# Four norms' residual rows in the middle turns: added by accumulating DMAs from GpSimd's queue instead of VectorE

## The chip, the cores and the metric

The kernel runs on one core of a Trainium2 chip. A core has TensorE (PE, matrix products), VectorE (DVE), ScalarE (ACT), GpSimd (POOL) and SyncE (SP). Each works through its own queue in order; semaphores tie the queues together. SP, ACT and POOL can issue DMAs, which 16 DMA engines carry out. The metric is the device time in microseconds (us) of one execution; several executions give a median. A separate profiled execution gives the page and the trace.

## The reference

A batch of 64 graphs with 256 nodes and 256 features, in float32, passes through two layers. Layer 0 is a graph attention layer with two attention steps; layer 1 is multi-head attention in which the adjacency matrix selects one of two value projections. Each layer ends in a feed-forward part, and each has two layer norms.

```python
# layer 0
h = _gat(x, adj, W1, a1, Fout)
h = _gat(h, adj, W2, a2, W2.shape[1])
h = _layernorm(residual + h, g_ln1, b_ln1)
residual2 = h
ff = jnp.matmul(jax.nn.relu(jnp.matmul(h, w_ff1) + b_ff1), w_ff2) + b_ff2
return _layernorm(residual2 + ff, g_ln2, b_ln2)
...
# layer 1
x = _ln(src + attn_out, g1, beta1)
ff = jax.nn.gelu(x @ W1 + b1, approximate=False) @ W2 + b2
return _ln(x + ff, g2, beta2)
```

A layer norm here is (x - mean) / sqrt(variance + eps), times a row g, plus a row b. There are four norms in all.

## The kernel before

**Tiles.** Two graphs make one unit, so there are 32 units. A unit's rows are a tile `y` of 128 partitions x 4 blocks x 256 float32 numbers, that is 512 KB. The pool has four such buffers.

**Norms.** What a norm feeds on goes two ways. The normalised rows, without g and b, are transposed and go into the next product, whose weights have g and b folded in. The residual path needs the rows with g and b. So after a norm `y` is normalised in place (L855 on ACT, L852 on GpSimd for two blocks of one of the norms), VectorE transposes it (L694), and later VectorE multiplies `y` by the row g (`times`, L864) and adds the row b (`plus`, L867), each as one instruction of 128 x 1024 elements. The rows rb1, rb2 and rb3 also hold the bias of the product that follows, which is added to the same residual. Then the products' results are added into `y` from PSUM: L995 for a feed-forward part, L814 for an attention.

**Turns.** `turn(u, u + 1, u + 2)` runs 32 times and works at once on three units at different stages: Y (`y_`) in layer 1, X (`x_`) in the second half of layer 0, and Z (`z`) in the first half of layer 0. Z exists in turns 0 to 29. A fourth unit, the one whose layer 1 ended in the turn before, is in `waiting`: its last norm is finished in this turn and its rows are stored. So each middle turn applies four pairs of g and b:

- rg1, rb1 to X's rows after its first norm (L1343, L1344); next read by the first L995 of X's feed-forward part.
- rg4, rb4 to the waiting rows (L1419); next read by the store to HBM (`stored`, L1202, on SP).
- rg3, rb3 to Y's rows after layer 1's first norm (L1444); next read by the first L995 of Y's feed-forward part, late in the same turn.
- rg2, rb2 to X's rows after layer 0's last norm (L1490); next read by L814 in the next turn.

**Order.** Inside a turn the order on PE, SP, VectorE and ACT is the order of the code (`manual_schedule`). GpSimd's order is chosen by the scheduler. SP issues, in this order within a turn: 12 DMAs that place transposed features (`hT<-yt`, L713) for X's first norm, 8 loads of x (L436), 6 more L713 (ACT issues another 6), the store of the waiting rows (L1202), the load of new rows into the buffer just stored (L441), 12 DMAs L703 for the next transposed features, and 8 loads of the adjacency (L449). GpSimd, in a turn, computes reciprocal square roots (`rs`, L837 and L838), copies the diagonal blocks of the transposed features (L711, L703), normalises two blocks (L852), and keeps small running checks (L780, L840, L1125). The products of a feed-forward part are done by a seven-product scheme over quarters (class `HiddenOut`), whose sums of quarters (L973) and additions into `y` (L995) are VectorE's. The softmax of Z (L768, L775, L779) and the scaling of its features by `z` (L791, ACT) lie in the same stretches; the product `ygp` (L811) uses them.

Of the kernel before, what the change touches and what calls it, by code (L numbers as in the profile page):

```python
# [12 lines left out]
ALU = mybir.AluOpType  # L13
# [372 lines left out]
def narrow_path(  # L386
# [13 lines left out]
    nc = tc.nc  # L400
# [102 lines left out]
    def row(v, name, t=None):  # L503
        n = v.shape[0]
        if t is None:
            t = const.tile([P, n], F32, name=name)
        nc.sync.dma_start(t, bass.AP(tensor=v.tensor, offset=v.offset, ap=[[0, P], [1, n]]))
        return t
# [41 lines left out]
    rg1, rb1, rg2, rb2 = row(g_g1, "rg1"), row(g_b1, "rb1"), row(g_g2, "rg2"), row(g_b2, "rb2")  # L550
# [14 lines left out]
    rg3, rb3, rg4, rb4 = row(t_g1, "rg3"), row(t_be1, "rb3"), row(t_g2, "rg4"), row(t_be2, "rb4")  # L565
# [289 lines left out]
            mark["normed"] = nc.scalar.activation(y[:, t, :], y[:, t, :], AF.Identity,  # L855
                                                  bias=nm[:, t:t + 1], scale=rs[:, t:t + 1])

    def affine(y, g_, b_):

        times(y, g_)  # L860
        plus(y, b_)

    def times(y, g_):
        nc.vector.tensor_mul(y, y, g_[:, None, :].to_broadcast(list(y.shape)))  # L864

    def plus(y, b_):
        nc.vector.tensor_add(y, y, b_[:, None, :].to_broadcast(list(y.shape)))  # L867

    def hidden_seven(u, l, hT, w, bi, func, d, tt):

# [135 lines left out]
    class Projections:  # L1006
# [17 lines left out]
        def out(s, x, o, b):  # L1024
            if x == "q":
                return s.qk[:, o, :, b * N:(b + 1) * N]
            return s.v[:, b * NB:(b + 1) * NB, o * F:(o + 1) * F]
# [172 lines left out]
    def stored(u, y, bt):  # L1200
        b = slice(G * u + bt.start // NB, G * u + bt.stop // NB)
        nc.sync.dma_start(out[b].rearrange("b (c p) f -> p (b c) f", p=P), y[:, bt, :])  # L1202

    def finish(u, y, b):

        normed(u, 3, y, range(b * NB, (b + 1) * NB))
        bt = slice(b * NB, (b + 1) * NB)
        affine(y[:, bt, :], rg4, rb4)
        stored(u, y, bt)
# [16 lines left out]
    def turn(y_, x_, z):  # L1226
        Y, X, Z = (g.get(u) for u in (y_, x_, z))
        hT, y = Y["hT"], Y["y"]
# [7 lines left out]
        def scores(n, heads=range(HPB)):  # L1236
            pe[n], e[n] = weighted(y_, *quads[n], q, k_, Y["aT"])
            powers(n, heads)
# [34 lines left out]
        with order:  # L1273
# [67 lines left out]
            first("4a 7b rb")  # L1341
            if X:
                times(X["y"], rg1)  # L1343
                plus(X["y"], rb1)  # L1344
            scores(3)
            first("sa sb", 2)
            masks(3)
# [64 lines left out]
            if not Z:  # L1412
                piece()
                hT = to_features(y, f"h3T{y_}")
                hT = [h.rearrange("p (t a r) -> p t a r", t=T, r=32) for h in hT]
                if not X:
                    affine(y, rg3, rb3)
            if waiting:
                affine(waiting[0][1], rg4, rb4)  # L1419
                stored(*waiting.pop(), slice(0, T))  # L1420
            if z + 1 < NG:
                load_rows(z + 1)
# [18 lines left out]
                offsets(*n)  # L1441
                applied_norm(X["y"], *n, [0])
            if Z:
                affine(y, rg3, rb3)  # L1444
            second("3a")
            if X:
                applied_norm(X["y"], *n, [1])
# [39 lines left out]
            Z["m"].shares()  # L1487
            Z["m"].scaled(F)
            out(3)
            affine(X["y"], rg2, rb2)  # L1490
            out(7)
            Z["n"] = norm(z, 0, Z["y"], mv=second_sums(z))
            out(4)
# [2 lines left out]
    waiting = []  # L1496

    with tc.manual_schedule(engines={mybir.EngineType.PE, mybir.EngineType.SP}):
# [34 lines left out]
        for u in range(NG):  # L1533
            turn(u, u + 1, u + 2)
# [54 lines left out]
```

## Time and profile before

| | us |
|---|---|
| median of 3 runs (lowest, highest) | 3045.75 (3045.45, 3047.17) |
| the profiled execution's own time | 3043.91 |
| its span in the trace | 3042.3 |
| one addition L867 of 128 x 1024, median | 1.226 |
| one multiplication L864 of 128 x 1024, median | 1.217 |
| DMA of 512 KB from SP, issue to landing: row load L441 / store L1202, median | 4.4 / 2.9 |
| DMA of 512 KB from GpSimd (L462, two at the start), issue to landing | 8.0 and 9.9 |
| time of those two on GpSimd's queue | 1.01 and 0.79 |

The page's rows give a group of instructions as line, engine, operation, tiles written and read, shape and count; then busy time in us and the mean of one in ns; then the idle time of the engine just before them and what ended most of it. The granted TensorE clock was 0.995 of full speed in the mean. A turn in the middle lasts about 92.4 us.

### The profile page before, as it was taken

To read this page: it belongs to the slowest core of one execution; us is meant where nothing else is said; L and a number is where in the kernel's file an instruction comes from. 1 tells how busy PE (TensorE), PEld (TensorE's weight loads), DVE (VectorE), ACT (ScalarE), POOL (GpSimd) and SP (SyncE) were. 2 spreads that over 40 slices of the span, in tenths; PEclk is the share of its full clock that TensorE was granted. 3 is DMA by queue.
4 is the path that set the end of the run, shared out by engine and by line. 5 is a ranking of instruction groups with operands and counts; after the bars stand their busy time and mean duration, and the time that the engine had idled before them with its cause. 6 is when DMAs were issued, how large, how long until landed. Compare 5 with 4: busy or idle time off the path is not lost.

```text
span 3042.3 us, 58414 instructions
## 1 busy us (share of the span) xinstructions
PE 3000.0 (99%) x22192; PEld 2459.6 (81%) x22192; DVE 2645.7 (87%) x5025; ACT 1684.9 (55%) x3404; POOL 679.8 (22%) x930
## 2 busy tenths in 40 slices
PE   7999999999999999999999999999999999999998
PEld 6788888888787888787888878887878887878876
DVE  5788988888898889898889888898988898988887
ACT  4455555655655555555555455556555555555553
POOL 4222221222211222212222112222112222122211
PEclk8999999999999999999999999999999999999999
DMA  5011111211111211111111112111112111121000
GB/s 147 13 35 36 37 39 25 44 37 39 34 35 32 44 37 39 33 27 43 40 37 36 40 25 44 38 39 33 34 35 44 36 38 35 25 45 37 19 13 16
DMA packets 428402, 113.24 MB, mean 37 GB/s; under 512 B 364586, under 2 KB 427604, under 8 KB 428116
## 3 DMA queue, kind: packets, MB, share of 16 engines
q1 hardware_dynamic: 418076, 102.20, 15.3%
q10 hardware_dynamic: 8984, 6.19, 0.8%
q8 instruction: 178, 2.92, 0.4%
q0 software_dynamic: 1056, 1.05, 0.1%
q14 instruction: 108, 0.88, 0.1%
HBM read 56.78 MB, written 16.78 MB: 24 GB/s over the span
## 4 chain that ended last, share of the span: by engine, by line
PE 90%; DVE 7%; ACT 1%; DMA 1%; POOL 1%; issue 0%; SPq 0%; DVEq 0%; POOLq 0%; ACTq 0%
PE yf L987 22%; PE h1a L898 15%; PE h1b L898 12%; PE po L1112 8%; PE qk L1053 7%; PE v L1053 7%; PE sp L1084 4%; PE xpp L740 4%; PE yop L811 4%; PE ygp L811 3%; PE zo L1115 2%; PE hpp L800 2%; DVE s L775 2%; DVE yt L694 1%; DVE eaq L973 1%; DVE y L995 1%
## 5 line engine op out<-in xcount | busy, mean ns | idle before, releaser
L907 ACT COPY h<-h1b 128x512 f32<-128x512 f32 x384 | 224.5, 585 | 349.4 <-PE h1b L898 342.6
L910 DVE TENSOR_TENSOR h<-h1a,h 128x512 f32<-128x512 f32 x384 | 262.9, 685 | 114.6 <-PE h1a L898 108.8
L1097 DVE TENSOR_TENSOR ea<-e,aT 128x1024 f32<-128x1024 f32 x256 | 311.2, 1237 | 2.9 <-ACT e L1093 2.6
L855 ACT ACTIVATE y<-y,nm,rs 128x256 f32<-128x256 f32 x450 | 249.8, 597 | 114.4 <-DVE nm L845 110.1
L1093 ACT ACTIVATE e<-sp 128x512 f32<-128x512 f32 x512 | 270.8, 600 | 28.1 <-PE sp L1084 21.4
L1036 ACT COPY qk<-qk 128x512 f32<-128x512 f32 x128 | 75.1, 587 | 339.0 <-PE qk L1053 339.0
L711 POOL COPY hT<-yt 32x256 f32<-32x256 f32 x244 | 203.2, 833 | 184.9 <-DVE yt L694 172.6
L837 POOL TENSOR_SCALAR rs<-mv 128x4 f32<-128x4 f32 (+1 forms) x134 | 33.3, 248 | 841.0 <-DVE mv L827 625.3
L826 DVE BATCH_NORM_STATS2 st<-y 128x6 f32<-128x256 f32 x512 | 207.3, 407 | 4.5
L995 DVE TENSOR_TENSOR y<-yf,y 128x256 f32<-128x256 f32 x448 | 183.2, 409 | 29.5 <-PE yf L987 29.4
L1125 POOL TENSOR_TENSOR low<-low,rq 128x16 f32<-128x16 f32 x64 | 13.9, 218 | 810.4 <-DVE rq L1124 810.4
L867 DVE TENSOR_TENSOR y<-y,rb 128x1024 f32<-128x1024 f32 (+1 forms) x130 | 167.0, 1284 | 3.2
L941 ACT ACTIVATE h<-h,cols 128x512 f32<-128x512 f32 x256 | 167.0, 714 | 1.5 <-DVE h L910 1.1
L864 DVE TENSOR_TENSOR y<-y,rg 128x1024 f32<-128x1024 f32 (+1 forms) x130 | 161.6, 1243 | 1.2 <-ACT y L855 1.1
L1102 DVE TENSOR_TENSOR es<-e 128x1024 f32<-128x1024 f32 x128 | 155.8, 1217 | 0.0
L703 POOL COPY hT<-yt 32x256 f32<-32x256 f32 x120 | 114.9, 958 | 169.3 <-DVE yt L694 165.1
L838 POOL TENSOR_TENSOR rs<-rs,mhalf 128x4 f32<-128x4 f32 (+1 forms) x134 | 146.9, 1096 | 8.3
L1084 PE MATMUL sp<-qk 32*128 32x256 f32 x2048 | 146.6, 400 | 0.4 <-DVE qk L1040 0.3
L742 ACT COPY xp<-xpp 128x260 f32<-128x260 f32 x128 | 45.4, 385 | 172.6 <-PE xpp L740 172.5
L694 DVE STREAM_TRANSPOSE yt<-y 128x256 f32<-128x256 f32 x364 | 136.0, 418 | 4.5
L1112 PE MATMUL po<-e,v 128*32 128x256 f32 x2048 | 136.3, 384 | 0.0
L898 PE MATMUL h1a<-tt,wf 128*128 128x256 f32 x512 | 134.2, 386 | 0.3 <-DVE h L910 0.3
(280 smaller groups left out, 7589.6 us busy)
## 6 DMA issues: line engine op xcount, KB each, us to landing
hT<-yt SPq DMA_DIRECT2D x912, 32.0 KB, 1.9
y<-in_x_dram SPq DMA_DIRECT2D x32, 512.0 KB, 4.5
xq<-in_x_dram SPq DMA_DIRECT2D x240, 64.0 KB, 2.1
aq<-in_adj_dram SPq DMA_DIRECT2D x240, 64.0 KB, 2.3
out_dram<-y SPq DMA_DIRECT2D x30, 512.0 KB, 2.9
hT<-yt ACTq DMA_DIRECT2D x180, 32.0 KB, 1.9
wf<-in_L_gnn_w_ff_dram SPq DMA_DIRECT2D x2, 1024.0 KB, 7.6
w<-in_L_gnn_W_dram SPq DMA_DIRECT2D x2, 1024.0 KB, 7.9
```

Source lines behind the costliest of these rows:

```text
L811: nc.tensor.matmul(ps[:, i * F:(i + 1) * F], lhs(t, k), rhs(b, k), start=(k == 0), stop=(k == n - 1))
L855: mark["normed"] = nc.scalar.activation(y[:, t, :], y[:, t, :], AF.Identity, bias=nm[:, t:t + 1], scale=rs[:, t:t + 1])
L898: nc.tensor.matmul(ps[:, i * N:(i + 1) * N], w_[:, f * P:(f + 1) * P], m, start=first and i == 0, stop=True, skip_group_check=True)
L907: mark["copied"] = nc.scalar.copy(out(h, o, b), pair(ps))
L910: mark["added"] = nc.vector.tensor_tensor(out(h, o, b), pair(one[h]), out(h, o, b), ALU.add)
L987: nc.tensor.matmul(s.ps[n][:, i * F2:(i + 1) * F2], a[:, k, i * P:(i + 1) * P], w_[:, k, :], start=n in (1, 2, 5) and i == 0 and k == 0, s ...
L995: mark["out"] = nc.vector.tensor_tensor(yq, s.ps[n][:, :F].rearrange("p (i f) -> p i f", i=NB), yq, ALU.add)
L1053: nc.tensor.matmul(ps[:, i * N:(i + 1) * N], l, r, start=n in (1, 2, 5) and i == 0, stop=True, skip_group_check=True)
L1084: nc.tensor.matmul(ps[a][:, j * N:(j + 1) * N], k_[hp, m, j0:j0 + P], q[hp, m, b * N:(b + 1) * N], start=True, stop=True)
L1093: nc.scalar.activation(e[:, a, :], ps[a], AF.Exp, scale=isd)
L1097: nc.vector.tensor_tensor(ea[:, a:a + 2, :], e[:, a:a + 2, :], ab[:, None, :].to_broadcast([P, 2, NB * N]), ALU.mult)
L1112: nc.tensor.matmul(po[hp, m * N:(m + 1) * N], vs[:, hp], w[:, a, j * N:(j + 1) * N], start=(n == 0), stop=(n == len(terms) - 1))
```

## The change

In turns that have a Z, the addition of the row b to `y` is a DMA that accumulates into `y`, issued from GpSimd's queue, in place of VectorE's `tensor_add`. Its source is the row tile of 128 x 256, read four times over. It applies to rb1, rb2, rb3 and rb4. The multiplications by g stay on VectorE. Turns 30 and 31, the part ahead of the turns and the halves of the last units (`finish`) keep VectorE's addition.

```diff
--- before.py
+++ after.py
@@ -855,16 +855,20 @@
             mark["normed"] = nc.scalar.activation(y[:, t, :], y[:, t, :], AF.Identity,
                                                   bias=nm[:, t:t + 1], scale=rs[:, t:t + 1])
 
-    def affine(y, g_, b_):
+    def affine(y, g_, b_, queue=False):
 
         times(y, g_)
-        plus(y, b_)
+        plus(y, b_, queue)
 
     def times(y, g_):
         nc.vector.tensor_mul(y, y, g_[:, None, :].to_broadcast(list(y.shape)))
 
-    def plus(y, b_):
-        nc.vector.tensor_add(y, y, b_[:, None, :].to_broadcast(list(y.shape)))
+    def plus(y, b_, queue=False):
+        rows_ = b_[:, None, :].to_broadcast(list(y.shape))
+        if queue:
+            nc.gpsimd.dma_start(y, rows_, accum_op=ALU.add)
+        else:
+            nc.vector.tensor_add(y, y, rows_)
 
     def hidden_seven(u, l, hT, w, bi, func, d, tt):
 
@@ -1341,7 +1345,7 @@
             first("4a 7b rb")
             if X:
                 times(X["y"], rg1)
-                plus(X["y"], rb1)
+                plus(X["y"], rb1, Z is not None)
             scores(3)
             first("sa sb", 2)
             masks(3)
@@ -1416,7 +1420,7 @@
                 if not X:
                     affine(y, rg3, rb3)
             if waiting:
-                affine(waiting[0][1], rg4, rb4)
+                affine(waiting[0][1], rg4, rb4, Z is not None)
                 stored(*waiting.pop(), slice(0, T))
             if z + 1 < NG:
                 load_rows(z + 1)
@@ -1441,7 +1445,7 @@
                 offsets(*n)
                 applied_norm(X["y"], *n, [0])
             if Z:
-                affine(y, rg3, rb3)
+                affine(y, rg3, rb3, True)
             second("3a")
             if X:
                 applied_norm(X["y"], *n, [1])
@@ -1487,7 +1491,7 @@
             Z["m"].shares()
             Z["m"].scaled(F)
             out(3)
-            affine(X["y"], rg2, rb2)
+            affine(X["y"], rg2, rb2, True)
             out(7)
             Z["n"] = norm(z, 0, Z["y"], mv=second_sums(z))
             out(4)
```

## The prediction

> **What bounds the kernel now.** I read the page first (shares, and the chain that ended last), then the busy time by windows, then TensorE's waits, and last one middle turn on every engine in order of time.
>
> ```profile
> span 3042.3 us, 58414 instructions
> PE 3000.0 (99%) x22192; PEld 2459.6 (81%) x22192; DVE 2645.7 (87%) x5025; ACT 1684.9 (55%) x3404; POOL 679.8 (22%) x930
> PE 90%; DVE 7%; ACT 1%; DMA 1%; POOL 1%; issue 0%; SPq 0%; DVEq 0%; POOLq 0%; ACTq 0%
> L867 DVE TENSOR_TENSOR y<-y,rb 128x1024 f32<-128x1024 f32 (+1 forms) x130 | 167.0, 1284 | 3.2
> ...
> 120.00:2860.00 2740.00, 2735.54 (x20419) 2245.89 (x20418) 2436.08 (x4612) 1546.53 (x3132) 603.54 (x824) 1.00 0.17 36
> ...
> PEld yf L987 <- DVE eaq L973: 15.0, 30, 0.5
> ```
>
> The windows line gives length, then busy time of PE, PEld, DVE, ACT and POOL. TensorE leaves only 2740.00 - 2735.54 = 4.5 us uncovered over the 30 middle turns that the change touches. VectorE, 87% busy, enters the chain at one place in a turn: a quarter sum (eaq, L973) that a product waits for, 0.5 us in each of 30 turns. One removed addition costs 1284 ns.
>
> Next, the turn from 1495.7 to 1588.1 us (VectorE, then GpSimd, then ACT and TensorE), and the transfers of the same size:
>
> ```profile
> 1530.56 1.22 DVE L867 TENSOR_TENSOR y<-y,rb 128x1024 f32<-128x1024 f32 x1
> 1544.68 0.42 DVE L995 TENSOR_TENSOR y<-yf,y 128x256 f32<-128x256 f32 x1
> 1548.25 0.42 DVE L995 TENSOR_TENSOR y<-yf,y 128x256 f32<-128x256 f32 x1 [0.48 <-PE yf L987]
> 1567.16 0.69 DVE L910 TENSOR_TENSOR h<-h1a,h 128x512 f32<-128x512 f32 x1 [1.00 <-PE h1a L898]
> 1575.74 0.41 DVE L995 TENSOR_TENSOR y<-yf,y 128x256 f32<-128x256 f32 x1
> ...
> 1552.10 4.40 POOL L711 COPY hT<-yt 32x256 f32<-32x256 f32 x4 [1.48 <-DVE yt L694]
> 1561.15 0.23 POOL L837 TENSOR_SCALAR rs<-mv 128x4 f32<-128x4 f32 x1 [4.65 <-DVE mv L827]
> 1563.64 2.95 POOL L852 TENSOR_SCALAR y<-y,rs,nm 128x256 f32<-128x256 f32 x2 [1.15 <-DVE nm L845]
> 1572.09 3.98 POOL L703 COPY hT<-yt 32x256 f32<-32x256 f32 x4 [5.50 <-DVE yt L694]
> ...
> 1581.65 1.71 ACT L791 ACTIVATE hp<-hp,z 128x256 f32<-128x256 f32 x4 [2.73 <-DVE z L779]
> 1582.84 3.62 PE L811 MATMUL ygp<-hp,s 128*128 128x256 f32 x16
> ...
> 2.87 0.79 POOL L462 DMA_DIRECT2D first<-in_adj_dram  x1
> ...
> out_dram<-y SPq DMA_DIRECT2D x30, 512.0 KB, 2.9
> first<-in_adj_dram POOLq DMA_DIRECT2D x2, 512.0 KB, 9.0
> ```
>
> The brackets are the idle time before an instruction and what ended it. VectorE waits for TensorE at 1548.25 and at 1567.16, so what it saves earlier in the turn turns into a longer wait there; from 1575.74 on it has no gap until after the masks, so a delay at that addition passes on. GpSimd has 4.65 and 5.50 us free where two of the new DMAs go.
>
> **What the Trainium skill says.** "DMA: Bandwidth & Descriptors", section "SWDGE vs HWDGE vs iDMA": an accumulating DMA can be issued from GpSimd alone, whose cores write its descriptors. No run shows such a DMA here; the plain ones of L462 occupied GpSimd for 0.79 and 1.01 us. "Perfetto Trace Analysis", section "DMA Instruction — SWDGE (GPSIMD)": that row ends when the descriptors are written, not when the data has landed. The trace agrees: rows of about 0.9 us, landing after 9.0. "Collectives: The Full Stack", section "The bandwidth ceiling: the fold count and why AG ≠ RS ≠ AR": an adding transfer reads two sources for each piece it writes and ran at half the copy's rate for that reason, not for the addition. No run here shows it. "SBUF — State Buffer", section "Who interferes with whom": a VectorE instruction with two SBUF inputs and a GpSimd instruction that reads SBUF block each other. The trace agrees: L852 takes 557 ns at its fastest and 1457 in the median.
>
> **The change part by part.** Turns 0 to 29 have a Z. Three norms (rb1, rb2, rb3) give 30 DMAs each, the fourth (rb4) needs a waiting result and gives 29: 119 of the 130 additions of L867 go, and 119 DMAs of 512 KB come. VectorE loses 119 x 1.284 = 152.8 us. The order of TensorE, ACT and SP is unchanged; VectorE's changes only in that the additions are gone and some short instructions around the turn's seam swap.
>
> Landing time of one such DMA, from GpSimd's start. From below: the store of the same size lands in 2.9 us. From above: a plain one from GpSimd took 9.9 us beside loads that filled the DMA engines (97% busy in the first 20 us); with a second read, 12. My value: 0.9 for descriptors, 2.9 as for the store, and once more the data time of 512 KB, which I estimate from the first page's "Anatomy of one DMA" (512 KB / 436 GB/s = 1.2): 5.0 us; 6 with other traffic. Time on GpSimd: 0.8 to 1.0 us by L462, up to 3 if the second read's descriptors are written one by one and more slowly; I take 1.
>
> rb1: multiplied until 1530.5, DMA right away (GpSimd is idle, an update of low waits behind it and nobody waits for that), landed at 1536.5; first reader is the L995 at 1544.68, 8 us later. The 1.22 us that VectorE saves here end in the wait at 1548.25. After it come only instructions that stay, up to eaq. Worth 0.
>
> rb4: GpSimd reaches it after the L711 copies at 1556.5. Behind it on GpSimd is the rs of L837 at 1561.15: free for 4.65 us, hidden. The store on SP waits for it: 1556.5 + 6 = 1562.5 instead of 1556.3; behind it on SP are the row load, which waits for the store to land (1562.5 + 2.9 = 1565.4 instead of 1559.1; its data is needed in the next turn), and then the transposed features' DMAs at 1572.0. They stay on time as long as the landing is under 1572.0 - 1556.5 - 2.9 - 0.4 (one issue) = 12.2 us. Worth 0; VectorE's gain ends in the wait for the features' DMAs at 1557.87 (L881).
>
> rb3: GpSimd reaches it after the two L852, at 1566.6, or some 0.9 sooner since the removed addition no longer blocks the second one (1457 to 557 ns). Behind it are the L703 copies, 5.5 us later. VectorE's gain ends in the wait at 1567.16. This landing has the nearest reader: L995 at 1575.74, 9.1 us after 1566.6. If it is late, z and the scaling at 1581.65 are, and with them ygp, whose second matmul (1582.84 + 0.22) needs the second scaled block (1581.65 + 2 x 0.43 = 1582.5): 0.5 us of slack. So nothing happens below 9.6 us, and beyond it TensorE loses the rest, 30 times. At 6 it is hidden, also when the later row load (1565.4 on) shares the engines and costs 1 to 2 us. Worth 0.
>
> rb2: multiplied until 1583.1, DMA then. Behind it is the rs of L837 at 1589.22, 6.1 us later. Landed near 1589; first reader is the attention's addition in the next turn, over 40 us later. VectorE gets to the moments of the next norm some 0.7 us sooner, but their first user, ACT's L855, stands behind a copy that waits for TensorE (1590.87). Worth 0.
>
> Less blocking between VectorE and GpSimd: a few tenths of a microsecond per turn on engines that wait anyway; I give it 1 us in the whole. Extra semaphore waits on VectorE: three a turn, some 0.02 us each as such rows show (17 to 21 ns), in places with slack. Sum: 0 - 1 = -1 us on the profiled execution's 3043.91 (span 3042.3 and 1.6 around it). The three runs' median lies 1.84 above it, so 3045.75 - 1 = 3045 after rounding.
>
> **The rivals.** B, the slower one: the accumulated rb3 lands late. Place: VectorE's L995 at 1575.74 in each of 30 turns. Price: each microsecond past 9.6 costs 30 us. For it: no row shows an accumulating DMA, 512 KB in 1 KB pieces read the destination too, and the row load now falls beside it. Against: quiet transfers of this size land in 2.9 to 4.5. At 11 us: 1.4 x 30 = 42, 3088; at the upper bound 12, 3118.
> C: GpSimd is held by the descriptors, so that rs, nm and the next turn's first norm are late at rb2's place. It decides from 6.1 + 0.6 (ACT's L855 starts 0.6 after nm is ready) = 6.7 us; at 8 us it costs 1.3 x 30 = 39, 3085. Against it: 0.79 to 1.01 us for 512 pieces.
> D, faster: the 0.5 us wait for eaq goes. At most 15.0 us, 3031. Against: the wait at 1548.25 lies between the removed addition and eaq.
> E: the additions that stay (11 of 130) or an order that eats the saving; the orders show that 119 are gone, so only a slow cause that I do not see is left here.
>
> **How the numbers follow.** About 0.2% (6 us) is what a measurement of this kernel can tell from no change. Hidden (A): 0.52, of it 0.42 within 6 us, 0.03 faster and 0.07 slower by small sharing of the DMA engines (0.2 to 0.4 us a turn, 6 to 12 us). B 0.28, C 0.12, D 0.06, E 0.02 and slower. Faster 0.03 + 0.06 = 0.09; same 0.42; slower 0.07 + 0.28 + 0.12 + 0.02 = 0.49. The likeliest case is A with 3045, its own range 3039 to 3057. The range of all: below 3038 lies part of D (0.04); above, it must take in B up to 11 us and C up to 8: 3095 leaves out about 0.12.
>
> **What would show it.** Right: L867's line down to 11 executions and VectorE near 2493 us busy, TensorE's span the same, GpSimd's DMA rows near 1 us, landing under 9 us, longer VectorE waits for TensorE at L995 and L910. Wrong: VectorE or TensorE waiting for a DMA into y at the second half's first L995; the L703 DMAs on SP starting late; nm waiting over 1.25 us for rs; or the wait for eaq shrinking.

## The result, and the profile after

| | before | after |
|---|---|---|
| median of 5 runs (lowest, highest), us | 3045.48 (3045.21, 3047.17) | 3058.97 (3050.12, 3063.02) |
| ratio to before, 95% interval | | 1.0042 [1.0024, 1.0061] |
| profiled execution, us (span) | 3043.91 (3042.3) | 3058.72 (3057.0) |

The change makes the kernel 13.5 us slower. The forecast of 3045 was wrong. The time lies within the stated range, on the slower side, but the loss sits in a place to which the prediction had given no cost. The runs after also spread over 12.9 us, against 2.0 before.

Lines behind L867 stand four later in the kernel after (L898 is L902 there), and the new DMA is L869. First the page of the kernel after: span, engines, the DMA queue that carries the new DMAs, their row on GpSimd, and their landing. Then the windows view over the middle turns: length, and busy time of PE, PEld, DVE, ACT and POOL.

```profile
span 3057.0 us, 58773 instructions
PE 3000.8 (98%) x22192; PEld 2460.1 (80%) x22192; DVE 2521.5 (82%) x4906; ACT 1683.6 (55%) x3404; POOL 768.5 (25%) x1049
...
q0 software_dynamic: 63888, 63.45, 13.0%
...
L869 POOL DMA_DIRECT2D y<-rb x119 | 158.4, 1331 | 358.7 <-ACT e L1097 307.9
...
y<-rb POOLq DMA_DIRECT2D x119, 512.0 KB, 5.3
```

```profile
120.00:2870.00 2750.00, 2733.94 (x20399) 2243.46 (x20398) 2310.42 (x4486) 1543.52 (x3128) 688.98 (x938) 1.00 0.31 58
```

The DMAs are what the prediction took them for: 1.33 us on GpSimd, landing after 5.3. VectorE has lost 124 us of busy time. TensorE's work is the same, but in the middle turns it is uncovered for 2750.00 - 2733.94 = 16.1 us, where it was 4.5. Its waits in that stretch say for what:

```profile
PE h1b L902 <- DMA hT<-yt: 11.8, 6, 2.5
PEld yf L991 <- DVE eaq L977: 15.2, 30, 0.5
```

The wait for eaq is what it was. New is a wait of h1b, a product of the feed-forward part, for the transposed features hT that it reads: six times (five of 2.2 to 2.5 us, one of 0.2), and not in 30 turns. The loss is an event of a few turns. The turns show it most plainly. From the first SP issue of L713 (in the middle of the turn) to that of the next turn, 92.40 us pass in a plain turn; in five turns it is 94.96, 97.18, 94.87, 94.99 and 94.87. Their excess sums to 14.9 us, as much as the whole difference of the two profiled executions (3058.72 - 3043.91 = 14.8). A few other turns take 0.1 to 0.4 us more than a plain one, but they do so in both kernels.

One of those five, in the timeline of SP, GpSimd and TensorE, and then the chain of waits through it:

```profile
1277.70 5.31 SPq L713 DMA_DIRECT2D hT<-yt  x6
1286.95 0.41 SPq L1206 DMA_DIRECT2D out_dram<-y  x1
...
1277.69 3.50 POOL L711 COPY hT<-yt 32x256 f32<-32x256 f32 x4 [1.49 <-DVE yt L694]
1281.13 1.35 POOL L869 DMA_DIRECT2D y<-rb  x1
...
1282.84 1.95 PE L991 MATMUL yf<-wf2t,h 128*128 128x128 f32 x16
1287.31 2.04 PE L902 MATMUL h1b<-hT,w 128*128 128x256 f32 x4 [2.52 <-DMA hT<-yt]
```

```profile
1278.26 2.00 SPq L713
1280.26 0.04 issue
1280.31 0.73 SPq L713
1281.04 0.04 issue
1281.09 0.60 SPq L713
1281.69 0.04 issue
1281.73 0.61 SPq L713
1282.35 0.04 issue
1282.39 4.57 DMA hT<-yt
```

The reader is to see four things. One of SP's six issues takes 2.00 us and not 0.6, so the issue of the last piece of hT starts at 1282.39 and its row ends at 1283.01 (1277.70 + 5.31), over a microsecond later than in a plain turn (3.93 us for the six). The accumulating DMA's row on GpSimd lies from 1281.13 to 1282.48, so its 512 KB reach the DMA engines just ahead of that piece. The last piece, 32 KB that lands in 1.9 us in the median, needs 4.57 us from its issue, and lands when the big block is through (the store, which waits for that block, is issued at 1286.95). TensorE has nothing else in its queue.

A plain turn, 352.79 us into the same execution, has the same DMA at the same distance, but SP's six issues are over in time, and h1b starts without a wait:

```profile
352.79 3.93 SPq L713 DMA_DIRECT2D hT<-yt  x6
...
356.23 1.34 POOL L869 DMA_DIRECT2D y<-rb  x1
...
359.71 1.03 PE L902 MATMUL h1b<-hT,w 128*128 128x256 f32 x4
```

The stretched issue is not new. In the kernel before nine turns of 30 take 4.5 us or more for SP's six issues, after seven. Before, it costs nothing: the large transfer in that place is the store, which stands behind hT in the same SP queue. The same turn before:

```profile
1274.75 5.21 SPq L713 DMA_DIRECT2D hT<-yt  x6
1280.07 0.52 SPq L1202 DMA_DIRECT2D out_dram<-y  x1
...
1281.67 1.03 PE L898 MATMUL h1b<-hT,w 128*128 128x256 f32 x4
```

The DMA view of that stretch (1274 to 1290 us, 40 slices of 0.4 us; tenths of the DMA engines' time, then GB/s), after and then before:

```profile
DMA  0000000000204000053334399999999000299920
GB/s 0 0 0 0 0 0 0 20 0 20 41 15 120 18 8 3 10 133 92 92 92 103 72 177 197 174 197 205 200 202 172 13 0 0 74 381 389 381 85 0
```

```profile
DMA  0000234363320005319993000704999000000000
GB/s 0 0 20 0 72 92 105 100 151 85 82 72 8 8 15 133 92 54 387 387 384 110 0 0 0 41 0 146 384 381 341 18 0 0 0 0 0 0 0 0
```

The accumulating block holds the engines for eight or nine slices at some 200 GB/s. The store before holds them for about three at 387, and hT is through by then.

### The profile page after: what moved, and what is told of

Same layout as the page of the kernel before. It is cut to its first block, busy times and chain, and to the rows that moved or that the text cites. A ratio compares the mean times of both kernels' runs of the same rounds, so it can differ in the third digit from the quotient of the medians.

```text
span 3057.0 us, 58773 instructions
## 1 busy us (share of the span) xinstructions
PE 3000.8 (98%) x22192; PEld 2460.1 (80%) x22192; DVE 2521.5 (82%) x4906; ACT 1683.6 (55%) x3404; POOL 768.5 (25%) x1049
## 4 chain that ended last, share of the span: by engine, by line
PE 89%; DVE 7%; DMA 2%; ACT 1%; issue 1%; SPq 1%; POOL 1%; ACTq 0%; POOLq 0%; DVEq 0%
PE yf L991 22%; PE h1a L902 15%; PE h1b L902 12%; PE po L1116 8%; PE qk L1057 7%; PE v L1057 7%; PE sp L1088 4%; PE xpp L740 4%; PE yop L811 4%; PE ygp L811 3%; PE zo L1119 2%; PE hpp L800 2%; DVE s L775 1%; DVE yt L694 1%; DVE y L999 1%; DVE eaq L977 1%
## 5 line engine op out<-in xcount | busy, mean ns | idle before, releaser
L1101 DVE TENSOR_TENSOR ea<-e,aT 128x1024 f32<-128x1024 f32 x256 | 311.5, 1238 | 15.5 <-ACT e L1097 15.1
L869 POOL DMA_DIRECT2D y<-rb x119 | 158.4, 1331 | 358.7 <-ACT e L1097 307.9
L999 DVE TENSOR_TENSOR y<-yf,y 128x256 f32<-128x256 f32 x448 | 184.1, 411 | 65.0 <-PE yf L991 64.6
L711 POOL COPY hT<-yt 32x256 f32<-32x256 f32 x244 | 176.9, 725 | 198.0 <-DVE yt L694 190.4
L703 POOL COPY hT<-yt 32x256 f32<-32x256 f32 x120 | 114.6, 955 | 159.3 <-DVE yt L694 155.1
L838 POOL TENSOR_TENSOR rs<-rs,mhalf 128x4 f32<-128x4 f32 (+1 forms) x134 | 136.9, 1021 | 8.3
L902 PE MATMUL h1a<-tt,wf 128*128 128x256 f32 x512 | 134.3, 386 | 0.3 <-DVE h L914 0.3
L1116 PE MATMUL po<-ea,v 128*32 128x256 f32 x2048 | 134.3, 379 | 0.0
```

The lines of the kernel that those rows point to most:

```text
L902: nc.tensor.matmul(ps[:, i * N:(i + 1) * N], w_[:, f * P:(f + 1) * P], m, start=first and i == 0, stop=True, skip_group_check=True)
L999: mark["out"] = nc.vector.tensor_tensor(yq, s.ps[n][:, :F].rearrange("p (i f) -> p i f", i=NB), yq, ALU.add)
L1101: nc.vector.tensor_tensor(ea[:, a:a + 2, :], e[:, a:a + 2, :], ab[:, None, :].to_broadcast([P, 2, NB * N]), ALU.mult)
L1116: nc.tensor.matmul(po[hp, m * N:(m + 1) * N], vs[:, hp], w[:, a, j * N:(j + 1) * N], start=(n == 0), stop=(n == len(terms) - 1))
```

## The experiments

The theory after this reading: only rb4's DMA costs time, by its arrival on the DMA engines while the last pieces of hT are still to be handed over. The rivals: any accumulating DMA costs a share of the DMA engines (1), GpSimd is held while it issues the DMAs (2), VectorE's freed time is worth something and the DMAs cost more than the difference shows (3), the later store and row load hold up SP (4). Each kernel was timed beside the kernel before on the same chip; there the kernel before took 3044.32 us in the first four, 3044.07 in the last three, which ran on another chip. The ratios are to these.

**rb4 back on VectorE.**

```diff
-                affine(waiting[0][1], rg4, rb4, Z is not None)
+                affine(waiting[0][1], rg4, rb4)
```

> Only rb4's addition goes back to VectorE; rb1, rb2 and rb3 stay accumulating DMAs (90 of 119). Theory (the rb4 DMA alone costs time, because its data come between the last pieces of the transposed features hT of L713 in the turns where one issue on SP takes 2 us in place of 0.6): 3045 to 3048 us, no wait of TensorE's h1b for hT. Rival 1 (any accumulating DMA costs its share of the DMA engines): 3/4 of 13.5 us stay, about 3055. Rival 2 (GpSimd held by descriptors): also about 3055.

Measured: 3042.14 us, ratio 0.9992 [0.9984, 1.0001]. Ninety accumulating DMAs cost nothing that can be told. Rivals 1 and 2 fall: the queue still carries 3/4 of the traffic, and GpSimd is still held 90 times.

**rb4 alone as a DMA.**

```diff
-                plus(X["y"], rb1, Z is not None)
+                plus(X["y"], rb1)
...
-                affine(y, rg3, rb3, True)
+                affine(y, rg3, rb3)
...
-            affine(X["y"], rg2, rb2, True)
+            affine(X["y"], rg2, rb2)
```

> Only rb4's addition is an accumulating DMA (29 of 119); the other three are on VectorE. Theory: the whole loss is here, 3055 to 3063 us, with some 5 waits of over 2 us of TensorE's h1b for hT. Rivals 1 and 2: 1/4 of the loss, about 3049.

Measured: 3055.13 us, ratio 1.0032 [1.0021, 1.0044], 10.8 us over before: most of the loss, at the lower edge of the expected range, with four waits of over 2 us in its trace (some five were expected). A turn's stall, with the same stretched issue (1651.57 to 1656.72) ahead of it:

```profile
1651.57 5.15 SPq L713 DMA_DIRECT2D hT<-yt  x6
...
1655.01 1.37 POOL L869 DMA_DIRECT2D y<-rb  x1
...
1660.91 1.10 PE L902 MATMUL h1b<-hT,w 128*128 128x256 f32 x4 [2.26 <-DMA hT<-yt]
```

The interval of the change (1.0024 to 1.0061) and this one overlap; whether rb1 to rb3 add anything to rb4's loss can't be told from these two, and by the run before they add nothing on their own.

**The additions left out.**

```diff
         if queue:
-            nc.gpsimd.dma_start(y, rows_, accum_op=ALU.add)
+            pass
```

> The 119 additions are left out: neither VectorE nor a DMA adds those rows. It prices VectorE's freed time (some 125 us busy) alone. Theory (nothing on the path waits for these additions): 3044 to 3046 us. Rival 3 (the freed time is worth something and the DMAs cost that much more): down to 3031, at most the 15 us that TensorE waits for the quarter sum eaq.

Measured: 3043.31 us, ratio 0.9995 [0.9987, 1.0003]. VectorE's freed time is worth nothing that can be told. Rival 3 falls, and with it the reason to make the change at all.

**rb4's DMA behind the features.** In turns with a Z the multiplication, the DMA, the store and the row load move as they are; in the others they stay.

```diff
-            if waiting:
-                affine(waiting[0][1], rg4, rb4, Z is not None)
-                stored(*waiting.pop(), slice(0, T))
-            if z + 1 < NG:
-                load_rows(z + 1)
+            if not Z:
+                if waiting:
+                    affine(waiting[0][1], rg4, rb4, Z is not None)
+                    stored(*waiting.pop(), slice(0, T))
+                if z + 1 < NG:
+                    load_rows(z + 1)
...
             second = hidden_seven(y_, 1, hT, w1s, b1, AF.Gelu, Y, tt.rearrange("p a n -> p (a n)"))
+            if Z:
+                if waiting:
+                    affine(waiting[0][1], rg4, rb4, Z is not None)
+                    stored(*waiting.pop(), slice(0, T))
+                if z + 1 < NG:
+                    load_rows(z + 1)
```

> All four stay accumulating DMAs, but rb4's multiplication (and so its DMA, the store and the row load behind it) stands in VectorE's order behind the subtractions that wait for the features hT, so that its data can't be in flight before hT has landed. Theory: 3045 to 3048 us, no wait of h1b over 1 us. Rivals 1 and 2 (traffic or GpSimd in general): about 3059 as in the change. Rival 4 (the later store and row load hold up SP's next features): slower than the change.

Measured: 3043.70 us, ratio 0.9997 [0.9989, 1.0006], with all 119 accumulating DMAs in place. A turn with a stretched issue (5.34 us for the six), in which the DMA starts when h1b already runs:

```profile
2014.45 5.34 SPq L713 DMA_DIRECT2D hT<-yt  x6
2029.95 0.41 SPq L1206 DMA_DIRECT2D out_dram<-y  x1
...
2024.76 1.35 POOL L869 DMA_DIRECT2D y<-rb  x1 [7.72 <-DVE y L999]
...
2021.64 1.10 PE L902 MATMUL h1b<-hT,w 128*128 128x256 f32 x4
```

Rival 4 falls as well: the store is 15.5 us behind SP's first issue here, later than in the change (9.25), and nothing is lost.

**Half of rb4's block.** From here on rb1 to rb3 are on VectorE.

```diff
-            nc.gpsimd.dma_start(y, rows_, accum_op=ALU.add)
+            h = T // 2
+            nc.gpsimd.dma_start(y[:, :h], rows_[:, :h], accum_op=ALU.add)
+            nc.vector.tensor_add(y[:, h:], y[:, h:], rows_[:, h:])
```

> As with rb4 alone as a DMA, but the DMA adds only blocks 0 and 1 (256 KB); VectorE adds blocks 2 and 3. Theory (the last piece of hT lands only when the accumulating DMA's data are through, so a stall is as long as what is left of them): at some 200 GB/s the block takes 1.3 us less, each stall falls from 2.3 to about 1.0 us and TensorE's clock doesn't fall: about 5 x 1.0 = 5 us over before, 3047 to 3051. Rival (it is the presence of a DMA on this queue, its issue or its completion, not its length): 3055 as with the whole.

Measured: 3044.86 us, ratio 1.0003 [0.9995, 1.0011]; the landing is 3.7 us and not 5.2. The rival in its plain form (a DMA's presence is enough) falls, but the expected 3 to 7 us did not come either. The trace shows a second thing that the edit changed: VectorE's half addition lengthens the L711 copies from 3.50 to 3.87 us, so the DMA starts some 0.4 us later behind SP's first issue (1648.99 - 1645.19 = 3.80, against 1655.01 - 1651.57 = 3.44). This run therefore doesn't separate length from start.

**A plain copy in place of the addition.**

```diff
-            nc.gpsimd.dma_start(y, rows_, accum_op=ALU.add)
+            nc.gpsimd.dma_start(y, rows_)
```

> As with rb4 alone as a DMA, same place, size and waits, but a plain copy: the residual is overwritten by the row and not added to. Theory (length of the block in flight decides): a plain block of 512 KB flows at twice the accumulating one's rate (store: 385 against 200 GB/s), so about as with the half one, 3047 to 3051. Rival (it is the adding itself, reading and writing back the destination): 3044 to 3046, no loss.

Measured: 3052.47 us, ratio 1.0028 [1.0018, 1.0039], 8.4 us over before and 1.5 above the expected range. The stalls are there without any adding, so it isn't the adding itself. They are shorter: the profile puts six waits of h1b down to hT, of 0.26 to 1.31 us. One of them:

```profile
1648.04 4.98 SPq L713 DMA_DIRECT2D hT<-yt  x6
...
1651.47 0.84 POOL L869 DMA_DIRECT2D y<-rb  x1
...
1656.08 1.10 PE L902 MATMUL h1b<-hT,w 128*128 128x256 f32 x4 [0.95 <-DMA hT<-yt]
```

The block ends sooner (landing 3.5 us after GpSimd's start, not 5.2), but it also arrives 0.5 us sooner, as its row on GpSimd is 0.84 us and not 1.37. That more turns still have pieces of hT to come then is borne out further below, turn by turn; that the loss is above the expected range for this reason alone is not shown.

**rb4's DMA later.**

```diff
+            nc.gpsimd.tensor_scalar(y, y, 1.0, 0.0, op0=ALU.mult, op1=ALU.add)
             nc.gpsimd.dma_start(y, rows_, accum_op=ALU.add)
```

> As with rb4 alone as a DMA, but GpSimd multiplies the rows by 1 first (128 x 1024, about 1.2 us), so the DMA starts that much later and is otherwise the same. Theory (what matters is whether the last pieces of hT are already on the DMA engines' queues when the block arrives; a late issue ends 0.5 us or less after the block's arrival): no loss or nearly none, 3044 to 3047. Rival (the DMA's mere overlap with hT's landing and with the products after it): 3053 to 3058.

Measured: 3042.77 us, ratio 0.9997 [0.9989, 1.0005]. The same DMA, of the same length (landing 5.2), with a multiplication of 1.04 us ahead of it on GpSimd, loses nothing. In a turn with a stretched issue it starts 4.91 us behind SP's first issue, not 3.44, and its data meet no piece of hT that is still to be handed over:

```profile
1274.28 4.78 SPq L713 DMA_DIRECT2D hT<-yt  x6
...
1277.85 1.04 POOL L869 TENSOR_SCALAR y<-y 128x1024 f32<-128x1024 f32 x1
1279.19 1.37 POOL L870 DMA_DIRECT2D y<-rb  x1 [0.30 <-POOL y L869]
...
1281.20 1.03 PE L903 MATMUL h1b<-hT,w 128*128 128x256 f32 x4
```

Against rb4 alone (1.0021 to 1.0044) this shows that the start decides: 1.5 us of start time (4.91 - 3.44), with the landing time unchanged, is the whole loss. The change itself had moved the start the wrong way: without VectorE's addition the L711 copies, which GpSimd runs just ahead of the DMA, take 3.50 us and not 4.40, so GpSimd reaches the DMA 0.9 us sooner.

**The stalls turn by turn.** SP's six issues take different times in different turns, so the traces above also show the mechanism without an edit. In the change and with rb4 alone the DMA's row on GpSimd ends 4.8 us behind SP's first issue. All nine turns there with 4.9 to 5.3 us for the six issues have a stall of h1b of 2.2 to 2.6 us, the three with 4.7 to 4.8 us one of 0.2 to 0.5, and no turn with 4.6 us or less has one of over 0.02. With the plain copy, whose row ends at 4.3 us, stalls begin at 4.3: its five turns with 4.3 to 4.6 us have 0.3 to 0.7 us. With the later DMA the row ends at 6.3 us, the six issues never take more than 5.1, and no stall is over 0.02. Kernels with no DMA for rb4 have at most 0.3 us in such turns.

## Why the prediction was wrong, point by point

**What bounds the kernel: right.** TensorE bounds it, and VectorE's waits at L995 and L910 swallow what it saves. The additions left out altogether give 1.0 us less (interval -4.0 to +0.9), where the prediction had -1. Two readings were loose, without harm to the argument. The chain on the page gives VectorE 7% of the span and not one place in a turn; what has one place is the wait of TensorE's weight loads for eaq. And the 152.8 us that VectorE was to lose are the sum of the rows of the additions: its busy time fell by 124, as neighbouring rows overlap (an addition from 1554.94 to 1556.24, the next instruction from 1556.16).

**rb1, rb3, rb2 worth 0: right.** With these three as DMAs the ratio is 0.9992 [0.9984, 1.0001]. The landing was put at 5.0, or 6 with traffic; it measured 5.3 in the median, 7.3 at most. The prediction took from the Trainium skill ("Collectives: The Full Stack", section "The bandwidth ceiling: the fold count and why AG ≠ RS ≠ AR") that an adding transfer runs at half the copy's rate because it reads two sources. The rate agrees with this case: some 200 GB/s against the store's 385, and against 264 to 422 of the plain copy in the same place. The reason is not shown here, as the two also differ in packets: 528 for the accumulating DMA, 144 for the plain one. The time on GpSimd was put at 1 us and measured 1.33.

**rb4: the step that failed.** The prediction put it as "VectorE's gain ends in the wait for the features' DMAs at 1557.87 (L881)" and "Worth 0". It looked at what waits behind the new DMA on GpSimd and on SP, and at what the later store does to the queue behind it. It put at nothing, without a reason, what the block's data do to transfers of another queue that are in flight, though it named the very wait. Two terms hid it. SP's issues were seen in one plain turn (3.93 us for six), while the trace of before has single L713 rows of up to 1994 ns beside a median of 589, and turns of 5.2 us. And the DMA's start was put at 1556.5, 4.4 us behind SP's first issue at 1552.1, with the L711 copies at their old length; the prediction shortened a GpSimd row for the missing addition at rb3, but not here. The start measured was 3.4. So the block's data arrive at 3.4 + 1.3 = 4.8 us, ahead of a last piece whose issue ends at 5.2. With the predicted start they would have arrived at 4.4 + 1.3 = 5.7 us, behind it: an estimate from these rows, which no run tried (the run with a start of 4.9 lost nothing).

The runs showed in place of "Worth 0": 2.2 to 2.5 us of stall in five turns of the profiled execution, and with the slower clock after one of them 14.8 us there; 10.8 us in the median with rb4 alone. None of the signs of being wrong that the prediction lists came: eaq waits as before, nm waits at most 1.2 us for rs, the L703 DMAs start 19.9 us behind SP's first L713 in a plain turn of either kernel, and no addition into y (L999 in the kernel after) waits for a DMA.

**The rivals.** B (rb3 lands late) and C (descriptors hold GpSimd) did not occur: 5.3 us against B's threshold of 9.6, and 1.33 against C's 6.7. D (the wait for eaq goes) did not occur: 15.2 us after, 15.0 before. What occurred was nearest to the small part of case A, "small sharing of the DMA engines (0.2 to 0.4 us a turn, 6 to 12 us)" with a chance of 0.07. That the sum comes near (13.5 us) is luck: it is not a small loss in each turn but a large one in a few, and the prediction showed no place for it.

**Extra waits on VectorE: nothing seen.** Plain turns last 92.40 us before and after.

No version here beats the kernel before by an amount that can be told; the best, rb4 back on VectorE, has an interval up to 1.0001.

## What to carry to other kernels

A large transfer on a queue of its own has no place behind the small transfers of another queue. Here the store stood behind hT on SP and did no harm; the accumulating block, on GpSimd's queue, came ahead of hT's last pieces. So for each DMA on a new queue, list what is in flight on the other queues when its data arrive, who waits for the last of those, and how much later that last one can be issued in the worst turn, not the median one. Where a large block needn't be early, let it wait for the small transfers that matter. And price the freed engine first: leaving the work out altogether shows in one run whether there is anything to gain.

## What the runs showed that I had not expected

**After a stall of 2 us TensorE can run slower.** In the turn at 1277 us the excess is 4.78 us, though the stall is 2.52. The two groups after it take 2.04 and 1.79 us:

```profile
1287.31 2.04 PE L902 MATMUL h1b<-hT,w 128*128 128x256 f32 x4 [2.52 <-DMA hT<-yt]
1289.15 1.79 PE L902 MATMUL h1a<-hT,w 128*128 128x256 f32 x4
```

```profile
1287.00:1288.00 1.00, 0.69 (x2) 0.63 (x3) 0.69 (x2) 0.00 (x0) 0.00 (x0) 0.64 0.08 30
1288.00:1289.00 1.00, 1.00 (x4) 0.81 (x3) 1.00 (x4) 0.00 (x0) 0.00 (x0) 0.50 1.08 384
1289.00:1290.00 1.00, 1.00 (x3) 0.72 (x3) 0.93 (x4) 0.58 (x1) 0.00 (x0) 0.50 0.32 111
1290.00:1291.00 1.00, 1.00 (x5) 0.85 (x4) 0.34 (x2) 0.00 (x0) 0.37 (x2) 0.66 0.10 16
```

Without a stall these groups take 1.03 us each. The second fence, from the windows view, has the microseconds from 1287 to 1291: the granted clock (third figure from the end) falls to 0.50 there, where it is 1.00 just before and after. The other four stalls of that execution, 2.22 to 2.35 us, were not followed by it. With rb4 alone one of 2.32 us was (its h1b group took 2.04 us too), while others of 2.26 to 2.63 us were not. In the middle turns of the kernel before, of rb4 back on VectorE, of the plain copy and of the later DMA, no microsecond has a clock below 0.95. So it came only after such stalls, but not after each; what decides is open.

**Most turns repeat to 0.02 us.** Most turns last 92.38 to 92.42 us; eight of the 29 that can be read before last 92.5 to 92.8. So a loss of 0.4% can be traced to single turns.

**The stretched issue.** In six to nine of 30 turns, in every kernel here, one of SP's six issues takes 1.0 to 2.0 us in place of 0.6, and in most of these turns one of ACT's as well. They are largely the same turns in every trace: the 2nd, the 11th and the 30th (at about 258, 1090 and 2850 us) have it in all nine. The trace of before thus held the slow turns already. Why an issue stretches was not tried.
